# Layer norms turned by VectorE and DMA instead of TensorE, and modulations with the condition as the stationary side

## The chip, the core and the metric

The kernel runs on one core of a Trainium2 chip. A core has five engines with queues of their own: TensorE (matrix products and transposes through its 128x128 array, results into PSUM), VectorE (elementwise work, reductions, 32x32 block transposes), ScalarE (activation functions, copies), GpSimd (called POOL in the profile) and SyncE (SP), which here issues every DMA. Each engine works through its queue in the order of the program, and waits at the head of it for semaphores that others raise. The metric is the device time of one execution in microseconds.

## What is computed

Four blocks of a diffusion transformer follow each other on a batch of 16 samples of 256 tokens with 256 channels, in float32. A condition vector of 256 numbers per sample gives shifts, scales and gates; a context of 77 tokens per sample is attended to. Cut to what matters here:

```python
def ln(x):            # over the 256 channels
    return (x - mean(x)) * rsqrt(var(x) + eps)

# block 0: shift, scale and gate from cond; masked self attention, cross attention, MLP
x = x + g_sa  * (attn(ln(x) * w * (1 + sc) + sh, mask) @ W)
x = x + g_x   * (cross(ln(x) * w * (1 + sc) + sh, ctx) @ W)
x = x + g_mlp * mlp(ln(x) * w * (1 + sc) + sh)
# block 1: x + cross attention of a modulated norm; the context is normed and modulated too
# block 2: self attention (modulated, gated), cross attention (norm alone), MLP (modulated, gated)
# block 3: self attention and cross attention with rotary embedding, MLP; all modulated, no gate
```

with `shift, scale = split(c @ W_mod + b)` and `c` the condition or its silu. Each sample goes through ten norms, so there are 160 in all; nine of the ten kinds have a modulation, and a tenth modulation serves the context of block 1.

## The kernel before

All of x stays in SBUF: `x_sb` holds 16 samples, each as two tiles of 128 tokens by 256 channels, tokens on partitions. The projections need the normed sample with channels on partitions, `xT` (two tiles of 128 channels by 256 tokens).

There are six stages one after the other: attention of block 0 (tiles named a, ac), its MLP (b), the attentions of blocks 1 and 2 (cx, c, cc), the MLP of block 2 (d), the attentions of block 3 (e, ec), and its MLP (f). Within an attention stage some five samples are in work at once. Their number is set by the buffers `kq` (queries and keys, five). An attention consists of a norm, projections (L592, L644, L764), scores for the row maxima (L805, L817), the maxima on VectorE (L831, L835, L839), which are block-transposed, written to DRAM and read back as an extra row of the queries (L851 to L858), scores again for the exponentials (L902, ScalarE L914, L916), the product with the values (L925), a division (L934 to L951) and the output projection with the residual (L972 to L990). An MLP of a sample is a norm, L1015, an activation (L1020) and L972.

The order of the instructions is not written by hand. Every step is entered as a task (`add`, L87) with an engine, a planned duration, the tasks it depends on, and the buffers it takes or uses (`Hold`); `Order.solve` (L104) starts tasks in order of planned time. On TensorE the task with the lowest priority number goes first, on the other engines the one that has been ready longest (with a head start for those that hold a PSUM bank), and a task starts only when its buffers are free by the numbers in `CAPS`. The result is one fixed order per engine. A DMA is a task on SP of 0.45 us (`ISSUE`), with a planned time to landing (`lat`, `mb`).

The norm is `norm_tasks` (L483): VectorE takes mean and variance (L467, L468), GpSimd makes the reciprocal deviation (L473, L474) and the normed sample `xn` (L495), TensorE turns it with four 128x128 transposes into a PSUM bank (L503), and ScalarE writes `xT` from the bank, with the scale and shift of the sample as its per-partition operands (L510, or a plain copy at L507). The modulation is `modulation` (L374): a DMA brings 256x512 weights into half a `kq` buffer (L380), TensorE makes shift and scale for all 16 samples with channels on partitions (L388), eight products in which a 128x128 block of the weights is the stationary side and the condition's 16 columns move, and VectorE adds the bias and the 1 (L393 to L398).

```python
pt = s["pt"] = psum(hm, NC)
for c in range(NC):
    for t in range(NT):
        nc.tensor.transpose(pt[:, c, t * P:(t + 1) * P], s["xn"][:, t, c * P:(c + 1) * P], ident)
```

Of the kernel before, what the change touches and what calls it, by code (L numbers as in the profile page):

```python
# [10 lines left out]
F32 = mybir.dt.float32  # L11
# [202 lines left out]
def pixart_kernel(ctx: ExitStack, tc: tile.TileContext, x, cond_t, ctx_in, mask_c, mask_s, tables, vecs, rows,  # L214
# [6 lines left out]

    CAPS = {"b": 8, "xn": 1, "xT": 2, "kq": 5, "v": 5, "mx": 3, "mr": 2, "ec": 2,
            "ts": 2, "oT": 2, "rope": 2, "qk": 4, "tmp": 2, "gb": 3, "wa": 1, "ctx": 2,
            "cin": 2, "bias": 2, "small": 4, "csmall": 2}

    const = ctx.enter_context(tc.tile_pool(name="const", bufs=1))
    wpool = ctx.enter_context(tc.tile_pool(name="weights", bufs=1))
# [49 lines left out]
    mrs, vs = [], []  # L277
    for j in range(CAPS["mr"]):
        mrs.append(dram.tile([2, 2, 4, 512], F32, name=f"mrow{j}"))

    for j in range(CAPS["v"]):
        vs.append(const.tile([P, NT, H, 32], F32, name=f"vt{j}"))
# [89 lines left out]
    gate_d, gate_t = {}, {}  # L372

    def modulation(name, src, col, shift_at, scale_at, c_t, bias, norm=None, gate=None, deps=(), prio=0, gprio=None):  # L374
        hw, hm, s = Hold("kq"), Hold("b"), {}
        m = mods[name] = const.tile([P, 4, B], F32, name=f"mod_{name}")

        def load():
            s["w"] = kqs[hw.no][:, 0]
            nc.sync.dma_start(s["w"], src[:, :, col:col + 512])  # L380

        def mults():
            ps = psum(hm)
            s["ps"] = ps[:, 0:4 * B].rearrange("p (s b) -> p s b", b=B)
            for i, at in enumerate((shift_at, scale_at)):
                for c in range(NC):
                    for k in range(NC):
                        nc.tensor.matmul(s["ps"][:, 2 * i + c, :], lhsT=s["w"][:, k, at + c * P:at + (c + 1) * P],  # L388
                                         rhs=c_t[:, k, :], start=(k == 0), stop=(k == NC - 1))

        def take():
            v = vec[:, VOFF[bias]:VOFF[bias] + 4].unsqueeze(2).to_broadcast([P, 4, B])
            nc.vector.tensor_tensor(m, s["ps"], v, ALU.add)  # L393
            if norm is None:
                nc.vector.tensor_scalar_add(m[:, 2:4, :], m[:, 2:4, :], 1.0)
            else:
                for c in range(NC):
                    nc.vector.tensor_scalar(m[:, 2 + c, :], m[:, 2 + c, :], 1.0, vcol(norm, c), ALU.add, ALU.mult)  # L398
        t0 = add("SP", ISSUE, load, deps=deps, take=[hw], prio=prio, mb=0.5, lat=2.0)
        t1 = add("PE", 2.0, mults, deps=[t0], take=[hm], use=[hw], prio=prio)  # L400
        mod_t[name] = add("DVE", 0.6, take, deps=[t1], use=[hm], prio=prio)
        if gate is None:
            return
        prio = prio if gprio is None else gprio
        hg = Hold("b")
        g_row, rest = gate
        hr, hw2 = Hold("tmp"), Hold("kq")

        def load2():
            s["wg"] = kqs[hw2.no][:, 0]  # L410
            nc.sync.dma_start(s["wg"][:, :, 0:D], src[:, :, col + 512:col + 768])

        def rowmm():
            pg = s["pg"] = psum(hg)
            nc.tensor.matmul(pg[0:B, 0:D], lhsT=pick(ROW[g_row], B), rhs=row, start=True, stop=False)
            for k in range(NC):
                nc.tensor.matmul(pg[0:B, 0:D], lhsT=c_t[:, k, :], rhs=s["wg"][:, k, 0:D], start=False,
                                 stop=(k == NC - 1))
            if rest is not None:
                bias_row(pg[0:B, D:2 * D], B, *rest)  # L420

        def rowtake():
            d = gate_d[g_row]
            pg, g2 = s["pg"], work.tile([P, NT, D], F32, tag="tmp", bufs=CAPS["tmp"], name=f"g2_{name}")
            nc.vector.tensor_copy(g2[0:B, 0, :], pg[0:B, 0:D])
            if rest is not None:
                nc.vector.tensor_tensor(g2[0:B, 1, :], pg[0:B, D:2 * D], g2[0:B, 0, :], ALU.mult)
            s["g2"] = g2

        def rowout():  # L430
            n = 1 if rest is None else 2
            nc.sync.dma_start(gate_d[g_row], s["g2"][0:B, 0:n, :])
        gate_d[g_row] = dram.tile([B, 1 if rest is None else 2, D], F32, name=f"gate_{g_row}")
        more = () if rest is None or len(rest) == 1 else (rest[3], late_t)
        t2 = add("SP", ISSUE, load2, deps=[*more, *deps], take=[hw2], prio=prio, mb=0.25, lat=2.0)
        t2 = add("PE", 2.2, rowmm, deps=[t2], take=[hg], use=[hw2], prio=prio)
        t3 = add("DVE", 0.8, rowtake, deps=[t2], take=[hr], use=[hg], prio=prio)
        gate_t[g_row] = add("SP", ISSUE, rowout, deps=[t3], use=[hr], prio=prio, mb=0.03, lat=2.0)
# [40 lines left out]
    def join(tasks, prio=0):  # L479
        return add("NO", 0.0, lambda: None, deps=tasks, prio=prio)  # L480

    def norm_tasks(s, b, eps, mod, name, prio, deps=()):

        hs, hn, hm, ht = Hold("small"), Hold("xn"), Hold("b"), Hold("xT")

        def stats():
            s["mv"] = norm_stats(x_sb[:, b], P, NT, name)

        def rstd():
            s["rstd"] = rstd_of(s["mv"], P, NT, eps, name)  # L490

        def scale():
            xn = s["xn"] = work.tile([P, NT, D], F32, tag="xn", bufs=CAPS["xn"], name=f"xn_{name}")
            for t in range(NT):
                nc.gpsimd.tensor_scalar(xn[:, t, :], x_sb[:, b, t, :], s["mv"][:, t, 0:1], s["rstd"][:, t:t + 1],  # L495
                                        ALU.subtract, ALU.mult)

        def turn():
            pt = s["pt"] = psum(hm, NC)
            s["xT"] = work.tile([P, NC, N], F32, tag="xT", name=f"xT_{name}")  # L500
# [4 lines that stand above are left out]
        def take():  # L505
            if mod is None:
                nc.scalar.copy(s["xT"], s["pt"])  # L507
            else:
                for c in range(NC):
                    nc.scalar.activation(s["xT"][:, c, :], s["pt"][:, c, :], AF.Identity,  # L510
                                         scale=mods[mod][:, 2 + c, b:b + 1], bias=mods[mod][:, c, b:b + 1])
        t1 = add("DVE", 1.0, stats, deps=[x_done[b], *deps], take=[hs], prio=prio)
        t2 = add("POOL", 0.95, rstd, deps=[t1], use=[hs], prio=prio)
        t3 = add("POOL", 2.5, scale, deps=[t2], take=[hn], use=[hs], prio=prio)
        t4 = add("PE", 4 * TR, turn, deps=[t3], take=[hm, ht], use=[hn], prio=prio)
        t5 = add("ACT", 0.6 if mod is None else 1.1, take, deps=[t4, mod_t.get(mod)], use=[hm, ht], prio=prio)
        x_done[b] = t3
        return t5, ht

    def early_add(s, b, pre_add, prio):  # L520

# [164 lines left out]
        a = add("PE", NC * nt * TR, turn, deps=deps, take=[hm], use=[h_dst, *hq], prio=prio)  # L686
        return take(lambda: u["p"], a, [hm, h_dst], prio)

    state = {"mr": 0}

    def attention(b, name, n, wv, wkeys, h_w, w_t, eps, mod, half, biases, masked, pre_add, gate, prio, ctxs=None,
                  barrier=None, after=None, norm_deps=()):
# [19 lines left out]
                  joins=[("mx", nm), ("mr", nm)] +  # L712
                        [(i, (nm, g, kc)) for i in ("e", "av") for g in range(NC) for kc in range(nk)])
        admitted.append(x_t)
        xT_t, hx = norm_tasks(s, b, eps, mod, nm, prio, deps=[x_t])

        norms.append(xT_t)
        if self_:
# [631 lines left out]
```

## Time and profile before

| | |
|---|---|
| median of three runs | 2684.58 us (2683.35 to 2687.24) |
| profiled execution, its own time | 2684.49 us |
| its span, first to last instruction | 2682.7 us |
| TensorE busy | 2635.8 us, 98% |
| VectorE, ScalarE, GpSimd busy | 1542.2, 1240.1, 1065.7 us |
| granted TensorE clock, mean | 0.995 |
| norm transposes L503 | 640, 272 or 273 ns each as recorded |
| modulation products L388 | 160 records, 263 ns each in the middle |
| stages: a and ac, b, cx to cc, d, e and ec, f | 642, 239, 761, 232, 576, 233 us |
| DMA, mean | 22 GB/s, 60.25 MB |

In the profile's groups, PE is a matmul and PEld a load of the stationary side; the two overlap, and matmuls overlap each other, so that the duration of one is longer than what it adds to a series. A float32 product is recorded as two matmuls, a transpose as one. "Idle before" is the engine's idle time just before the instructions of a row, with what ended most of it. The chain that ended last is followed back from the last instruction; its shares add up to the span. Buffer numbers are left out of the names.

### The profile page before, as it was taken

How to read it: one execution, taken by the hardware profiler on the slowest of the kernel's cores; microseconds unless marked ns; L12 is line 12 of the kernel's file. 1: busy time of each engine (PE TensorE's matmuls, PEld its weight loads, DVE VectorE, ACT ScalarE, POOL GpSimd, SP SyncE). 2: the span in 40 equal slices, each digit the busy share in tenths (PEclk: the TensorE clock that was granted, in tenths of full speed). 3: DMA queues.
4: the chain of work that ended last, by engine and by line, in shares of the span. 5: the costliest groups of instructions: out<-in, count | busy, mean ns of one | idle time of the engine just before them, and what ended most of it. 6: DMA issues, size and time to landing. Idle time of an engine off the chain costs nothing.

```text
span 2682.7 us, 56475 instructions
## 1 busy us (share of the span) xinstructions
PE 2635.8 (98%) x22144; PEld 1887.2 (70%) x22144; DVE 1542.2 (57%) x4379; ACT 1240.1 (46%) x2495; POOL 1065.7 (40%) x1413
## 2 busy tenths in 40 slices
PE   8999999999999999999999999999999999999999
PEld 5656665766888667666666667888666666667888
DVE  7788886664320566766775664111788876883100
ACT  2444444664332456455555554232455555553332
POOL 4333332545443445133334544433333333562321
PEclk9999999999999999999999999999999999999999
DMA  4000000012110000100000012000000000000000
GB/s 145 14 7 9 10 7 14 16 52 90 31 39 12 25 17 6 35 13 13 20 16 9 5 33 66 16 20 16 11 4 4 4 3 6 5 21 24 20 20 20
DMA packets 53570, 60.25 MB, mean 22 GB/s; under 512 B 19592, under 2 KB 38264, under 8 KB 52536
## 3 DMA queue, kind: packets, MB, share of 16 engines
q1 hardware_dynamic: 53304, 56.65, 7.1%
q8 instruction: 174, 2.85, 0.4%
q14 instruction: 92, 0.75, 0.1%
HBM read 50.44 MB, written 6.19 MB: 21 GB/s over the span
## 4 chain that ended last, share of the span: by engine, by line
PE 92%; DVE 3%; POOL 2%; ACT 1%; issue 1%; DMA 1%; DVEq 0%; ACTq 0%; POOLq 0%; SPq 0%
PE bank L972 20%; PE bank L902 13%; PE bank L1015 12%; PE bank L925 11%; PE bank L805 7%; PE bank L592 7%; PE bank L644 6%; PE bank L764 5%; PE bank L503 3%; PE bank L817 2%; PE bank L684 2%; PE bank L895 2%; PE bank L388 1%; PE bank L579 0%; ACT e_ac L914 0%
## 5 line engine op out<-in xcount | busy, mean ns | idle before, releaser
L902 PE MATMUL bank<-kq 32*128 32x256 f32 (+1 forms) x5120 | 606.2, 396 | 2.9 <-DMA kq<-mrow 2.5
L902 PEld LDWEIGHTS bank<-kq 32*128 32x128 f32 (+1 forms) x5120 | 354.3, 168 | 158.4 <-issue 108.2
L805 PE MATMUL bank<-kq 32*128 32x512 f32 x1536 | 411.1, 638 | 1.9 <-DVE kq L617 1.8
L831 DVE CUSTOM_DVE_ANT_0 junk<-bank,ctxT_masks 128x256 f32<-128x256 f32 x448 | 188.7, 421 | 52.5 <-PE bank L805 21.4
L916 ACT ACTIVATE e_a<-bank 128x512 f32<-128x512 f32 x256 | 137.8, 597 | 175.0 <-PE bank L805 147.1
L916 ACT ACTIVATE e_e<-bank 128x512 f32<-128x512 f32 x256 | 136.1, 599 | 143.9 <-PE bank L805 105.2
L835 DVE TENSOR_REDUCE mx_c<-bank 128x2 f32<-128x512 f32 x256 | 160.2, 681 | 36.8 <-PE bank L805 36.2
L916 ACT ACTIVATE e_c<-bank 128x512 f32<-128x512 f32 x256 | 134.9, 601 | 100.3 <-PE bank L805 74.8
L835 DVE TENSOR_REDUCE mx_e<-bank 128x2 f32<-128x512 f32 x256 | 161.1, 681 | 26.5 <-PE bank L805 25.4
L978 DVE TENSOR_TENSOR x_sb<-x_sb,bank 128x512 f32<-128x512 f32 x80 | 54.8, 685 | 202.3 <-PE bank L972 193.4
L817 PE MATMUL bank<-kq 32*128 32x154 f32 x2048 | 166.9, 309 | 1.3 <-DVE mx_ec L839 0.5
L805 PEld LDWEIGHTS bank<-kq 32*128 32x128 f32 x1536 | 127.4, 184 | 25.2 <-issue 8.1
L817 PEld LDWEIGHTS bank<-kq 32*128 32x128 f32 x2048 | 130.0, 185 | 17.2 <-issue 6.8
L1020 ACT ACTIVATE h_d<-bank,vec 128x256 f32<-128x256 f32 x128 | 53.7, 471 | 156.0 <-PE bank L1015 105.8
L1020 ACT ACTIVATE h_f<-bank,vec 128x256 f32<-128x256 f32 x128 | 53.6, 471 | 153.4 <-PE bank L1015 132.2
L1020 ACT ACTIVATE h_b<-bank,vec 128x256 f32<-128x256 f32 x128 | 53.6, 471 | 146.2 <-PE bank L1015 118.6
L1015 PE MATMUL bank<-xT_b,kq 128*128 128x256 f32 x512 | 113.8, 379 | 0.0
L1015 PE MATMUL bank<-xT_d,kq 128*128 128x256 f32 x512 | 113.6, 380 | 0.0
L1015 PE MATMUL bank<-xT_f,kq 128*128 128x256 f32 x512 | 113.4, 379 | 0.0
L972 PE MATMUL bank<-kq,h_b 128*128 128x256 f32 x512 | 113.2, 379 | 0.0
L972 PE MATMUL bank<-kq,h_d 128*128 128x256 f32 x512 | 113.2, 379 | 0.0
L972 PE MATMUL bank<-kq,h_f 128*128 128x256 f32 x512 | 113.2, 379 | 0.0
(336 smaller groups left out, 5751.4 us busy)
## 6 DMA issues: line engine op xcount, KB each, us to landing
kq<-in_mod_dram SPq DMA_DIRECT2D x10, 512.0 KB
cin<-in_ctx_in_dram SPq DMA_DIRECT2D x36, 128.0 KB
x_sb<-in_x_dram SPq DMA_DIRECT2D x16, 256.0 KB
gb_b<-gate_g0m SPq DMA_DIRECT2D x16, 256.0 KB
gb_c<-gate_g2a SPq DMA_DIRECT2D x16, 256.0 KB
gb_d<-gate_g2m SPq DMA_DIRECT2D x16, 256.0 KB
out_dram<-x_sb SPq DMA_DIRECT2D x16, 256.0 KB
kq<-mrow SPq DMA_DIRECT2D x224, 16.0 KB
```

The source lines that it names most:

```text
L592: nc.tensor.matmul(dst[:, g, :], lhsT=w[:, k, g * P:(g + 1) * P], rhs=xT[:, k, :], start=(k == 0), stop=(k == NC - 1))
L644: nc.tensor.matmul(u["p"][0:r, at:at + D], lhsT=xT()[:, k, t * P:t * P + r], rhs=w()[:, k, :], start=(k == 0), stop=(k == NC - 1))
L805: ls.append(lambda ps=ps, R=R, keys=keys: nc.tensor.matmul(ps.rearrange("p (s k) -> p s k", k=N), lhsT=s["qx"][R, 0, g, t * P:(t + 1) * P] ...
L817: ls.append(lambda ps=ps, R=R, keys=keys, tt=tt: nc.tensor.matmul(ps[:, 2 * tt * n:2 * (tt + 1) * n].rearrange("p (s k) -> p s k", k=n), l ...
L831: nc.vector.tensor_tensor_reduce(junk, u[i][:, i2 * N:(i2 + 1) * N], mb[:, t, :], -1.0, 3.0e38, ALU.add, ALU.min, m[:, i2, g, t:t + 1])
L835: nc.vector.tensor_reduce(m[:, :, g, t], u[i].rearrange("p (s k) -> p s k", k=N), AX.X, ALU.max, negate=True)
L902: (lambda ps=u[i], R=R, q=q: nc.tensor.matmul(ps[0:rows_n, q * N:(q + 1) * N], lhsT=s["kz"][R, q, g, kc * P:kc * P + rows_n], rhs=s["qx"][ ...
L916: nc.scalar.activation(e, u[i][0:rows_n], AF.Exp)
L925: nc.tensor.matmul(u5["p"][32 * r:32 * r + 32, 1 - q, :], lhsT=s["v"][0:rows_n, kc, 8 * g + 2 * r + 1 - q, :], rhs=s["e", g, kc, r][0:rows ...
L972: nc.tensor.matmul(u["p"][:, t, :], lhsT=lhsT(k, t), rhs=w()[:, k, :], start=(k == 0), stop=(k == nk - 1))
L1015: nc.tensor.matmul(u["p"][:, j, :], lhsT=wv["w1"][:, k, f * P:(f + 1) * P], rhs=s["xT"][:, k, :], start=(k == 0), stop=(k == NC - 1))
L1020: nc.scalar.activation(s["h", i][:, j, :], u["p"][:, j, :], func, bias=vcol(b1, 2 * i + j))
```

## The change

The norm keeps its first three steps. Its fourth, the turn on TensorE, stays only where `direct` is true: for the self attention of block 0 and the first two samples (`BY_PE` is 2). Everywhere else four steps take its place. VectorE transposes `xn` in blocks of 32x32 into `y` (one buffer); SP writes `y` to a DRAM tile `yd` (two of them), 128 rows of 2 KB; SP reads it back into `xr` (one buffer) with the blocks in their places, four runs of 512 bytes per partition; and ScalarE writes `xT` from `xr`, in two instructions with or without a modulation. No PSUM bank is held, and `xT` is taken only at the last step.

In the modulation the condition's 16 columns become the stationary side, and the 512 columns of the weights move: two products in place of eight, with the 16 samples on partitions. ScalarE copies the 16x512 result to SBUF (a `tmp` buffer), and four transposes on TensorE bring it into the old layout in a second PSUM bank.

```diff
-        hw, hm, s = Hold("kq"), Hold("b"), {}
+        hw, hr_, hc, hm, s = Hold("kq"), Hold("b"), Hold("tmp"), Hold("b"), {}
...
         def mults():
-            ps = psum(hm)
-            s["ps"] = ps[:, 0:4 * B].rearrange("p (s b) -> p s b", b=B)
+            for k in range(NC):
+                nc.tensor.matmul(psum(hr_)[0:B], lhsT=c_t[:, k, :], rhs=s["w"][:, k, :], start=(k == 0),
+                                 stop=(k == NC - 1))
+
+        def copy():
+            s["r"] = work.tile([P, NT, D], F32, tag="tmp", bufs=CAPS["tmp"], name=f"mr_{name}")
+            nc.scalar.copy(s["r"][0:B].rearrange("b t d -> b (t d)"), psum(hr_)[0:B])
+
+        def turn():
+            s["ps"] = psum(hm)[:, 0:4 * B].rearrange("p (s b) -> p s b", b=B)
+            r = s["r"].rearrange("b t d -> b (t d)")
             for i, at in enumerate((shift_at, scale_at)):
                 for c in range(NC):
-                    for k in range(NC):
-                        nc.tensor.matmul(s["ps"][:, 2 * i + c, :], lhsT=s["w"][:, k, at + c * P:at + (c + 1) * P],
-                                         rhs=c_t[:, k, :], start=(k == 0), stop=(k == NC - 1))
+                    nc.tensor.transpose(s["ps"][:, 2 * i + c, :], r[0:B, at + c * P:at + (c + 1) * P], ident[0:B, 0:B])
...
-        t1 = add("PE", 2.0, mults, deps=[t0], take=[hm], use=[hw], prio=prio)
+        t1 = add("PE", 0.95, mults, deps=[t0], take=[hr_], use=[hw], prio=prio)
+        t1 = add("ACT", 0.6, copy, deps=[t1], take=[hc], use=[hr_], prio=prio)
+        t1 = add("PE", 0.4, turn, deps=[t1], take=[hm], use=[hc], prio=prio)
...
-        t4 = add("PE", 4 * TR, turn, deps=[t3], take=[hm, ht], use=[hn], prio=prio)
-        t5 = add("ACT", 0.6 if mod is None else 1.1, take, deps=[t4, mod_t.get(mod)], use=[hm, ht], prio=prio)
         x_done[b] = t3
-        return t5, ht
+        if direct:
+            t4 = add("PE", 4 * TR, turn, deps=[t3], take=[hm, ht], use=[hn], prio=prio)
+            return add("ACT", 0.6 if mod is None else 1.1, take, deps=[t4, mod_t.get(mod)], use=[hm, ht], prio=prio), ht
+
+        hy, hd = Hold("y"), Hold("yd")
+
+        def turn32():
+            s["y"] = work.tile([P, 4, NT * NC * 32], F32, tag="y", bufs=CAPS["y"], name=f"y_{name}")
+            nc.vector.transpose(s["y"].rearrange("p f (u i) -> p f u i", i=32),
+                                s["xn"].rearrange("p t (c j f) -> p f (t c) j", j=32, f=4))
+
+        def move_out():
+            s["yd"] = yds[state["yd"] % len(yds)]
+            state["yd"] += 1
+            nc.sync.dma_start(s["yd"], s["y"].rearrange("p f n -> p (f n)"))
+
+        def move_in():
+            s["xr"] = work.tile([P, 4, NT, NC, 32], F32, tag="xr", bufs=CAPS["xr"], name=f"xr_{name}")
+            nc.sync.dma_start(s["xr"].rearrange("p a t c i -> p a (t c i)"),
+                              s["yd"].rearrange("(a j) (f n) -> (j f) a n", j=32, f=4))
+
+        def take_in():
+            s["xT"] = work.tile([P, NC, N], F32, tag="xT", bufs=CAPS["xT"], name=f"xT_{name}")
+            for c in range(NC):
+                to = s["xT"][:, c, :].rearrange("p (t a i) -> p t a i", t=NT, a=4)
+                of = s["xr"][:, :, :, c, :].rearrange("p a t i -> p t a i")
+                if mod is None:
+                    nc.scalar.copy(to, of)
+                else:
+                    nc.scalar.activation(to, of, AF.Identity, scale=mods[mod][:, 2 + c, b:b + 1],
+                                         bias=mods[mod][:, c, b:b + 1])
+        hr = Hold("xr")
+        t = add("DVE", 0.7, turn32, deps=[t3], take=[hy], use=[hn], prio=prio)
+        t = add("SP", ISSUE, move_out, deps=[t], take=[hd], use=[hy], prio=prio, lat=2.0)
+        t = add("SP", ISSUE, move_in, deps=[t], take=[hr], use=[hd], prio=prio, lat=2.0)
+        return add("ACT", 1.1, take_in, deps=[t, mod_t.get(mod)], take=[ht], use=[hr], prio=prio), ht
...
-        xT_t, hx = norm_tasks(s, b, eps, mod, nm, prio, deps=[x_t])
+        xT_t, hx = norm_tasks(s, b, eps, mod, nm, prio, deps=[x_t], direct=masked and self_ and b < BY_PE)
```

`CAPS` gains `"y": 1, "yd": 2, "xr": 1`. Because the order is planned from the tasks, the order of every other instruction shifts as well.

## The prediction

> **What bounds the kernel now.** I read the page's first part and its chain, then the chain in order of time, then the row of the line that the change removes, then single moments of the timeline.
>
> ```profile
> PE 2635.8 (98%) x22144; PEld 1887.2 (70%) x22144; DVE 1542.2 (57%) x4379; ACT 1240.1 (46%) x2495; POOL 1065.7 (40%) x1413
> PE 92%; DVE 3%; POOL 2%; ACT 1%; issue 1%; DMA 1%; DVEq 0%; ACTq 0%; POOLq 0%; SPq 0%
> ```
>
> TensorE bounds it: it makes up 92% of the chain that ended last, and in all 40 slices but the first it is busy nine tenths. The removed transposes (L503) hold "PE bank L503 3%" of that chain, 2.5 to 3.5% of 2682.7 us or 67 to 94 us, waits in front of them included; the modulations (L388) hold 1%. What a norm's four transposes cost the array itself is read where nothing else happens, in an MLP stage:
>
> ```profile
> 2643.80 6.91 PE bank L972 x32
> 2650.71 6.91 PE bank L1015 x32
> 2658.05 6.91 PE bank L972 x32
> ```
>
> L1015 ends at 2657.62, and the next sample starts at 2658.05: the four transposes between them take 0.43 us. In the attention stages there is more around them:
>
> ```profile
> its engine sat idle before it (us, times) until:
>   issue: 18.6, 48
>   POOL xn_cx L495: 7.6, 4
>   POOL xn_b L495: 3.6, 4
>   POOL od_c L947: 3.5, 9
> ```
>
> This is L503's own view. "issue" is 0.39 us a time, where the array changes from 32-row tiles to full ones; the others are TensorE standing at the head of its queue until GpSimd has normalised.
>
> [...] L503's row shows 273 as one duration, but the 0.43 us for four show that they overlap, so I count 0.43. [...]
>
> ```profile
> 1161.28 0.32 SPq L540 DMA_DIRECT2D gb_c<-gate_g2a  x1
> 1175.33 0.53 SPq L854 DMA_DIRECT2D mrow<-mt_c  x1
> 1177.32 1.08 SPq L858 DMA_DIRECT2D kq<-mrow  x2
> 1164.34 1.27 POOL L528 TENSOR_TENSOR x_sb<-x_sb,gb_c 128x512 f32<-128x512 f32 x1 [1.77 <-DMA gb_c<-gate_g2a]
> ```
>
> A write to DRAM is followed by its read 1.99 us later; a 256 KB read is in use 3.06 us after its issue.
>
> **The change, part by part**, on the span of 2682.7 us.
>
> 1. Transposes. Ten norms for 16 samples are 160; two (stage a, b below BY_PE = 2) keep the old path. 158 x 0.43 = 68 us leave TensorE's queue. Every stage keeps TensorE above 97% busy, so this is on the path that sets the end: -68.
>
> 2. Waits and mode changes around them. The chain's share says 67 to 94 us, so up to 26 beyond the 68. The order of the changed program has 1391 changes of array mode against 1449; 58 fewer at 0.39 are 23, if none was hidden. Bounds 0 and 26; I take half: -13.
>
> 3. Modulations. Before: eight products in 16 records.
>
> ```profile
> 672.00 1.97 PEld L388 LDWEIGHTS bank<-scondT,kq 128*128 128x128 f32 x16
> 673.89 2.25 PEld L1015 LDWEIGHTS bank<-xT_b,kq 128*128 128x128 f32 x11
> 22.96 0.54 PEld L417 LDWEIGHTS bank<-kq,condT 128*16 128x16 f32 x4 [0.42 <-DMA x_sb<-in_x_dram]
> 23.93 3.32 PEld L644 LDWEIGHTS bank<-w_a,xT_a 128*128 128x128 f32 x16 [0.42 <-ACT xT_a L510]
> ```
>
> From the first weight load to the next line's: 1.89 us each. After: two products of 512 columns. The gate product L417 has the same stationary side and 256 columns: four records in at most 0.97 us (the next load waited for ScalarE as well). Twice the columns: at most 1.94, or 1.73 at the 0.216 of L1015 (6.91/32) per 256. Four small transposes add at most 0.43. So 2.16 to 2.37 against 1.89, times 10: +3 to +5; I take +3. The new ScalarE copy (as L507's 128x512 copy, 0.59) sits between the two TensorE steps; nine modulations are loaded long before use. For the first, the other input is late anyway: GpSimd's norm ends at 12.5 us, the modulation at 11.99 before.
>
> 4. VectorE gains one 128x512 block transpose per norm. L951's 128x256 takes 0.435 from SBUF, L934's 128x512 takes 0.71 from PSUM. The reading here steps by four elements, which no row shows; bounds 0.6 and 1.1, taken 0.71: 158 x 0.71 = 112 us, hidden where VectorE has room. Least room:
>
> ```profile
> 100.00:200.00 100.00, 99.13 (x892) 61.24 (x894) 84.64 (x343) 46.22 (x87) 35.01 (x42) 1.00 0.03 9
> ```
>
> The third number is VectorE: 85% in self-attention of stage a. One norm per 20 us or so adds 0.71, and the stage shortens by some 3%: about 90%. An in-order VectorE that full delays row maxima, whose banks TensorE wants. Bounds 0 and 20 us (all that stages a and ac save); taken +5.
>
> 5. ScalarE reads SBUF in place of PSUM, 2 x 0.567 before. [...] ScalarE is at 46%: 0.
>
> 6. The new chain. VectorE, write, read, ScalarE. A store of 256 KB has its packets done 1.8 us after issue (DMA packets under the out_dram issue), so the write is some 2.0 with the hand-over; the read 3.1 with 512-byte pieces (bounds 2.6 and 4.0); ScalarE 1.15; semaphores and short queueing 0.4. Sum 6.7 us from SP's issue of the write to xT. SP waits for the block transpose, then for the write, and everything behind on SP stands: the write of the row maxima and its read, gate loads, x stores. Each pays only if its own reader is close. SP issues 316 DMAs more, some 0.45 each, on top of some 550 at about 0.5: 420 us of 2600, not full.
>
> Is xT in time? In the changed program's order I sum, for each norm, the TensorE work issued between SP's write and the first matmul on xT, at the before-trace's rates (0.432 for a 256-column product, 0.125 for L902's, 0.137 for L925's, 0.244 for L805's). In the MLP stages it is 16 to 60 us. In the 110 attention norms the middle is 9.5; nine are under 6.7, the smallest 3.8 (c2), 4.2 (c3), 5.2. What is missing below 6.7 sums to 12 us: +12. The same count made for the row maxima of the kernel before, at their 5 us, says 6.7 us; the waits view says
>
> ```profile
> PEld bank L902 <- DMA kq<-mrow: 4.2, 7, 1.3
> PE bank L902 <- DMA kq<-mrow: 2.5, 3, 0.9
> ```
>
> so the count is good to a few us. For the row maxima after, it says 1 us. The waits for xT that exist before (L510's view: matmuls waited 4.0 + 3.0 + 2.9 + 2.3 + 1.4) go where the order no longer has them; I take -10 of these 14.
>
> 7. The PSUM bank that a norm held is freed, and xn (one buffer) is released by VectorE and not by TensorE's queue. POOL waited 137.5 us for L503 in the last MLP; that wait was off the path. 0.
>
> Sum: -68 - 13 + 3 + 5 + 12 - 10 = -71: span 2611.7. The profiled execution's time was 2684.49 with span 2682.7, 1.8 more, and equals the median of the runs (2684.58). Forecast 2613 us.
>
> **Rivals.**
> - A. The waits vanish whole: all 94 us of L503's share go and nothing new comes, 2684.5 - 94 + 3 = 2594, and without the old waits for xT 2584. For: the slack of 9.5 is more than 6.7. Against: nine norms are short.
> - B. VectorE becomes the bound in stages a and e, or the read takes 4 us (sum 7.6): the stalls are 21, not 12, and the VectorE loss 20, not 5. 2613 + 24 = 2637; with a round trip of 8.5 us (37 us of stall) 2653. For: 85% busy before, one in-order queue.
> - C. Slower: the round trip is late everywhere. The same count gives 55 us of stall at 9.0, 88 at 9.7, 105 at 10. The gain before stalls is 83 us (68 + 13 + 10 - 3 - 5), so it decides at 9.6 us, 2.9 more than I have, on every attention norm: SP, held at its head by row-maxima writes or by the block transpose behind VectorE's queue. At 10.5 us the count is 136: 2684.5 - 83 + 136 = 2738. For: the write of one norm and the row maxima alternate in SP's order. Against: the order already leaves 2.45 us for each hop, and TensorE work, not SP, sets the pace.
> - D. It changes nothing: only if transposes were hidden; the MLP chain, where they show as 0.43 gaps, excludes it.
>
> **Chances.** Forecast case (2595 to 2635) 0.62; A (below 2595) 0.12; B (2635 to 2679) 0.18; D (within 0.2%, 2679 to 2690, about what a measurement of this kernel can tell from no change) 0.02; C 0.06. Range for 8 in 10: leaving 0.08 below 2590 and 0.12 above 2655. Faster 0.92.
>
> **What would show it.** MLP periods of 13.82 us (14.25 - 0.43); no L503 rows but eight transposes; modulations of about 2.2 us on TensorE; VectorE's new row near 0.71 us; the read issued about 2 us after the write; TensorE's waits on xT some 12 to 16 us in the attention stages. It is wrong if TensorE's idle time before projections grows past 40 us, if SP's waits move row maxima onto TensorE's path, or if VectorE's maxima show as what ends TensorE's waits in stage a.

## The result and the profile after

The changed kernel takes 2703.7 us (median; 2695.8 to 2706.0) against 2685.8 us of the kernel before on the same chip: a ratio of 1.0062, 95% interval 1.0045 to 1.0079. It is slower by 18 us, where 2613 us was forecast. The profiled execution has a span of 2701.0 us against 2682.7.

The first part of the page and its chain, for the kernel after:

```profile
PE 2619.5 (97%) x21432; PEld 1818.7 (67%) x21432; DVE 1686.9 (62%) x4537; ACT 1256.4 (47%) x2521; POOL 1065.4 (39%) x1413
PE 69%; DVE 5%; DMA 2%; POOL 2%; ACT 1%; issue 1%; SPq 0%; DVEq 0%; ACTq 0%; POOLq 0%
```

TensorE has lost 712 of its 22144 matmul records but only 16 us of busy time; VectorE has gained 145 us. This chain breaks off in stage a: its shares add up to 80%, and the first 530 us are not in it, so that the 69% of TensorE can't be set beside the 92% of before. In the part that it covers, DMA holds 64 us, 58 of them the new writes and reads; the chain of before, over the whole span, held 18 us of DMA.

Several steps came out as forecast. In an MLP stage the chain in order of time shows the period of 2 x 6.91 = 13.82 us, without the 0.43 us gap (start, duration, instructions):

```profile
2590.00 6.91 PE bank L1059 x32
2596.91 6.91 PE bank L1016 x32
2603.82 6.91 PE bank L1059 x32
```

One round trip in stage c, from the timeline (start, duration, engine, line, operation; in brackets the idle time before it and what ended it):

```profile
1243.93 1.11 DVE L535 STREAM_TRANSPOSE y_c<-xn_c 128x512 f32<-128x512 f32 x1 [1.14 <-POOL xn_c L506]
1245.07 0.33 SPq L541 DMA_DIRECT2D yd<-y_c  x1
1247.13 0.37 SPq L545 DMA_DIRECT2D xr_c<-yd  x1
1249.70 1.09 ACT L556 ACTIVATE xT_c<-xr_c,mod_2a 128x256 f32<-128x256 f32 x2 [2.29 <-DMA xr_c<-yd]
1251.16 0.94 PEld L636 LDWEIGHTS bank<-xT_c,w_c 128*128 128x128 f32 x5 [0.45 <-ACT xT_c L556]
```

The read follows the write after 2.06 us, ScalarE follows 2.57 us later, and xT is there at 1250.79, 5.7 us after SP's write, where 6.7 was counted. That is one of the quick ones. Over the 110 attention norms on the new path the middle is 6.6 us, 54 take longer than 6.7, and ten longer than 9.6. A modulation holds TensorE for about 2.2 us, as forecast (the one at 700.48 us: 1.82 for the products, 0.35 for the turns). What was not as forecast is the first line: 1.11 us for a block transpose, not 0.71. It is so in every stage, as L535's own view shows for stage c (durations in ns, shortest, middle and longest):

```profile
L535 DVE STREAM_TRANSPOSE y_c<-xn_c x16: 1079/1108/1116, 1079.8 to 1396.0; 128x512 f32<-128x512 f32 x16
```

TensorE's instructions waited for xT as the views of L510 before and of L556 after list (us, times):

```profile
  PEld bank L592: 4.0, 8
  PEld bank L764: 3.0, 8
  PEld bank L925: 2.9, 8
  PEld bank L644: 2.3, 4
  PE bank L592: 1.4, 1
```

```profile
  PEld bank L636: 19.7, 28
  PE bank L636: 10.0, 6
  PEld bank L808: 3.4, 8
  PEld bank L969: 1.7, 5
  PEld bank L688: 1.3, 4
```

That is 36 us of waits for xT against 13.6 before, where 12 to 16 were expected. For 15.6 of the 26.1 us that loads (PEld) waited, earlier matmuls still ran, so not all of it is lost time.

By stage the span moved like this (boundaries at the first and last MLP product):

| stage | a | b | c | d | e | f |
|---|---|---|---|---|---|---|
| before | 641.9 | 239.2 | 760.5 | 232.2 | 575.8 | 233.1 |
| after | 665.7 | 240.7 | 758.2 | 229.8 | 577.9 | 228.6 |

Stage a alone loses 23.8 us. The others together gain 5.6.

One reading of the trace orders all that follows. I split the span into three: **gaps** (no matmul in execution), **half clock** (half of TensorE's busy time in stretches whose clock record says 0.5: an estimate of what those stretches cost; in the profile after, the matmuls of L636 follow each other there after 427 ns in the middle, and elsewhere after 216), and the **rest**, which is TensorE at work, with the short waits that its overlapping records hide.

| | span | gaps | half clock | rest |
|---|---|---|---|---|
| before | 2682.7 | 46.9 | 12.7 | 2623.2 |
| after | 2701.0 | 81.4 | 29.9 | 2589.7 |
| difference | +18.3 | +34.5 | +17.2 | -33.5 |

These are one profiled execution each, and executions of one kernel differ by some us. So TensorE did get less to do. The saving came back, and more, as gaps and as half clock. Here is one such place, first a line of the timeline of TensorE, then the windows of 3.4 us around it (PE's busy time is the number after the length; the granted clock is the third from the end):

```profile
1316.06 2.61 PE L636 MATMUL bank<-xT_c,w_c 128*128 128x256 f32 x8 [2.05 <-ACT xT_c L556]
```

```profile
1313.90:1317.40 3.50, 1.45 (x10) 1.07 (x7) 2.15 (x5) 2.00 (x5) 0.01 (x1) 1.00 0.25 70
1317.40:1320.80 3.40, 3.40 (x20) 1.83 (x22) 1.05 (x3) 2.06 (x5) 0.48 (x1) 0.50 0.33 82
1320.80:1324.20 3.40, 3.40 (x35) 2.23 (x30) 2.49 (x4) 2.17 (x4) 0.79 (x1) 1.00 0.00 0
```

xT is 2.05 us late; in the next 3.4 us TensorE, busy throughout, gets half its clock (20 matmuls, then 35). By estimate the wait of 2.05 us costs 3.75: its length and half of the 3.4 us.

### The profile page after: what moved, and what is told of

The parts are those of the page before. It is cut to its first block, busy times and chain, and to the rows that moved or that the text cites. A ratio compares the mean times of both kernels' runs of the same rounds, so it can differ in the third digit from the quotient of the medians.

```text
span 2701.0 us, 55663 instructions
## 1 busy us (share of the span) xinstructions
PE 2619.5 (97%) x21432; PEld 1818.7 (67%) x21432; DVE 1686.9 (62%) x4537; ACT 1256.4 (47%) x2521; POOL 1065.4 (39%) x1413
## 4 chain that ended last, share of the span: by engine, by line
PE 69%; DVE 5%; DMA 2%; POOL 2%; ACT 1%; issue 1%; SPq 0%; DVEq 0%; ACTq 0%; POOLq 0%
PE bank L1016 18%; PE bank L1059 12%; PE bank L946 9%; PE bank L969 8%; PE bank L636 6%; PE bank L849 5%; PE bank L808 3%; PE bank L688 3%; PE bank L861 2%; PE bank L728 1%; DMA xr_c<-yd 1%; DVE mx_e L879 1%; DMA yd<-y_c 1%; PE bank L386 0%; DMA yd<-y_b 0%
## 5 line engine op out<-in xcount | busy, mean ns | idle before, releaser
L946 PE MATMUL bank<-kq 32*128 32x256 f32 (+1 forms) x5120 | 613.1, 399 | 2.9 <-DMA kq<-mrow 0.6
L879 DVE TENSOR_REDUCE mx_c<-bank 128x2 f32<-128x512 f32 x256 | 159.7, 679 | 16.1 <-PE bank L849 15.1
L1059 PEld LDWEIGHTS bank<-xT_d,kq 128*128 128x128 f32 x512 | 97.0, 190 | 14.6 <-issue 1.6
```

The costliest lines, as they stand in the source:

```text
L879: nc.vector.tensor_reduce(m[:, :, g, t], u[i].rearrange("p (s k) -> p s k", k=N), AX.X, ALU.max, negate=True)
L946: (lambda ps=u[i], R=R, q=q: nc.tensor.matmul(ps[0:rows_n, q * N:(q + 1) * N], lhsT=s["kz"][R, q, g, kc * P:kc * P + rows_n], rhs=s["qx"][ ...
L1059: nc.tensor.matmul(u["p"][:, j, :], lhsT=wv["w1"][:, k, f * P:(f + 1) * P], rhs=s["xT"][:, k, :], start=(k == 0), stop=(k == NC - 1))
```

## The experiments

My theories after the result: 1, VectorE's longer block transpose delays row maxima and so the banks that TensorE wants; 2, the round trip makes xT late; 3, in the attention stages the transposes had not been what sets the pace; 4, added later, the planner's order is better or worse by accident; 5, added last, gaps cost clock.

### The transposes and the new path, in a fixed order

In these four the planner's input is unchanged, so every engine keeps its order and the instructions named are missing. Two of them also give `xn` three buffers in place of one: the first, in which ScalarE reads `xn` itself, and the one with the moves alone, in which SP writes `xn` itself; what those buffers alone are worth was not tested.

The kernel before without the transposes:

```diff
+            if name not in ("a0", "a1"):
+                s["pt"] = s["xn"]
+                return
             pt = s["pt"] = psum(hm, NC)
```

> The kernel before in its own order on every engine, with the 158 norms' transposes on TensorE left out; ScalarE takes the normalised tile itself in place of the turned one (so the values of everything behind are not the reference's), still after GpSimd has made it. It prices what the removed transposes are worth to the kernel before when nothing takes their place. Forecast's own theory (they lie on the path everywhere): 81 us less, about 2604 us. Theory 3 (only in the MLP stages TensorE sets the pace; in the attention stages the pace is set by the loop through VectorE and ScalarE that empties the banks): 48 x 0.43 = 21 us less, about 2664 us.

Measured: 2643.9 us, ratio 0.9848 (0.9832 to 0.9863): 41 us, half of the 81 of the forecast's steps 1 and 2 and twice what theory 3 said. The split (always of the profiled execution) says by stage where it paid:

| | transposes, at 0.43 us a norm | rest | gaps | half clock | span |
|---|---|---|---|---|---|
| MLP stages b, d, f (48 norms) | 20.6 | -19.2 | +0.1 | 0 | -19.1 |
| attention stages a, c, e (110 norms) | 47.3 | -41.8 | +11.3 | +11.8 | -18.7 |

In the MLP stages nearly the whole price is gained. In the attention stages most of the work does go, but more than half of that comes back, as gaps and as half clock, and some 6 us were hidden in TensorE's records from the start. How that can be hidden is seen where self-attention samples follow each other: six samples of self-attention in stage e, between the ends of the same two projections, look like this:

```profile
2030.80:2163.60 132.80, 132.69 (x1229) 87.43 (x1232) 106.33 (x222) 68.53 (x132) 44.50 (x60) 1.00 0.02 4
```

```profile
2006.20:2138.60 132.40, 132.02 (x1204) 85.53 (x1208) 106.36 (x222) 68.86 (x132) 44.42 (x60) 1.00 0.02 4
```

(windows of the kernel before, then of this one.) 24 transposes are gone and the stretch is 0.4 us shorter, not 2.6; and TensorE is "busy" for 99.9% of it with them and 99.7% without. The timelines of the same place in both:

```profile
2049.10 0.69 PE L503 MATMUL bank<-ident,xn_e 128*128 128x128 f32 x4
2049.16 0.76 POOL L947 TENSOR_TENSOR od_e<-ts_e,rec_e 128x128 f32<-128x128 f32 x2
2049.96 0.45 DVE L951 STREAM_TRANSPOSE oT_e<-od_e 128x256 f32<-128x256 f32 x1
2050.89 1.59 PEld L972 LDWEIGHTS bank<-w_e,oT_e 128*128 128x128 f32 x8 [0.43 <-issue]
```

```profile
2024.53 0.76 POOL L950 TENSOR_TENSOR od_e<-ts_e,rec_e 128x128 f32<-128x128 f32 x2
2025.32 0.45 DVE L954 STREAM_TRANSPOSE oT_e<-od_e 128x256 f32<-128x256 f32 x1
2026.25 1.59 PEld L975 LDWEIGHTS bank<-w_e,oT_e 128*128 128x128 f32 x8 [0.74 <-ACT xT_e L513]
```

The projection L972 (L975) starts 1.73 and 1.72 us after GpSimd's product with the reciprocals has started. That chain, GpSimd, VectorE, projection, keeps its own pace at this place, and the transposes had stood in its shadow. "POOL od_c L947" in L503's own view, which the prediction read as GpSimd's norm, is this product in stage c. Theory 3 holds here, not everywhere.

The changed kernel's order without the new path, as below; then with the block transposes put back alone, and with the moves put back alone, which then carry `xn`. In the first two, xT waits for nothing, not even for the norm:

```diff
         def turn32():
+            return
         def move_out():
-            nc.sync.dma_start(s["yd"], ...)
         def move_in():
-            nc.sync.dma_start(s["xr"]..., s["yd"]...)
+            s["xr"] = still...
```

> The changed kernel in its own order on every engine, with the block transposes on VectorE and both moves left out; ScalarE's copy into xT reads a tile that never changes (so the values are not the reference's), and xT waits for neither the norm nor the moves. It shows what the changed order would take if the new path cost nothing. Forecast's theory, and theories 1 and 2, which put the loss on VectorE's block transpose or on the round trip: about 2600 us (2585 to 2620). Theory 3 (the transposes were not what set the pace of the attention stages): 2655 to 2680 us.

> As the run before this one, with the block transposes put back on VectorE, where they cost their 1.10 us each and release the normalised tile, but without the moves and with xT waiting for none of it (values not the reference's). Theory 1 (VectorE's 174 us delay row maxima in its one queue and so the banks that TensorE wants): most of the loss is back, 2680 us or more. Theory 2 (the round trip through DRAM makes xT late): within 15 us of the run without them. Theory 3: some 20 to 30 us above the run without them.

> The changed kernel in its own order with the block transposes on VectorE left out and both moves kept: SP writes the normalised tile to DRAM and reads it back, and xT waits for that (the 32x32 blocks are not turned, so the values are not the reference's). Theory 1: near the run without both parts, within 15 us. Theory 2: close to the changed kernel, 2685 us or more. If both matter, the two single parts add up to what the changed kernel has more than the run without both.

| | time | ratio to before (95%) |
|---|---|---|
| neither | 2666.3 | 0.9932 (0.9910 to 0.9954) |
| block transposes | 2674.3 | 0.9961 (0.9946 to 0.9976) |
| moves | 2683.2 | 0.9995 (0.9986 to 1.0004) |
| both: the changed kernel | 2703.7 | 1.0062 (1.0045 to 1.0079) |

With a path that costs nothing the changed order is still 22 us slower than the order of before without transposes. That was in no theory. The block transposes cost 8, the moves 17, and together they cost 37, 12 more than their sum. The four times of "neither" run from 2660 to 2675 us, so the 22 and the 8 are good to some 6 us; the 12 are 10 when they are taken from the ratios, and with all four intervals good to some 9. It would fit that only with both does the block transpose delay the write, which is not shown. Neither theory 1 nor theory 2 alone gives the 37 us; theory 2 alone gives about half.

### The parts, and the planner's numbers

The old norms with the new modulations; the new norms with the old modulations; the new norms in the MLP stages only (with the old modulations); and the changed kernel with measured durations in its planner:

```diff
-        t = add("DVE", 0.7, turn32, ...
-        t = add("SP", ISSUE, move_out, ..., lat=2.0)
-        t = add("SP", ISSUE, move_in, ..., lat=2.0)
+        t = add("DVE", 1.1, turn32, ...
+        t = add("SP", ISSUE, move_out, ..., lat=1.5)
+        t = add("SP", ISSUE, move_in, ..., lat=2.4)
```

> The kernel before with the modulations changed and every norm turned by TensorE as before. Forecast: +3 us, 2688 us. If new tasks push the planner's order about, which the run without both parts suggests (22 us longer than the kernel before without its transposes, in the changed order), up to +20 us.

> The changed kernel with the old modulations (16 small products each) and the new norms. If the norms carry the loss: 2695 to 2710 us, as the changed kernel. If the new modulations carry the 22 us that the changed order loses: 2675 to 2685 us.

> The kernel before with the new path in the 48 norms of the MLP stages alone; the attention stages' norms are turned by TensorE, the modulations are the old ones. The runs so far give the MLP stages as the only place where a period falls by the transposes' whole 0.43 us (13.82 against 14.25), with 16 to 60 us of other work to cover the round trip: 19 us less, about 2666 us. If the planner's order of the attention stages is upset by it as well: 2675 us or more.

> The changed kernel with the planner told what the trace shows: 1.1 us for the block transpose in place of 0.7, and latencies that make the write 2.05 us and the read 2.85 us from issue to use. If the loss comes from an order written for a too cheap block transpose and too cheap a read: 2670 to 2685 us. If the loss is in the work itself, or the order moves by as much for any change of its inputs: within 10 us of the changed kernel, 2695 to 2715 us.

| | time | ratio (95%) | gaps | half clock | rest |
|---|---|---|---|---|---|
| modulations only | 2694.3 | 1.0034 (1.0021 to 1.0047) | 47.4 | 12.3 | 2636.6 |
| norms only | 2667.2 | 0.9935 (0.9920 to 0.9950) | 68.4 | 16.1 | 2578.4 |
| norms of the MLP stages only | 2680.9 | 0.9987 (0.9978 to 0.9996) | 54.0 | 32.5 | 2601.8 |
| changed kernel, planner's numbers | 2670.4 | 0.9944 (0.9927 to 0.9960) | 56.8 | 19.4 | 2591.8 |

The new norms alone make the kernel faster by 18 us; with the modulations, worth 9 us by themselves, they make it 18 us slower. And the whole change, with three numbers of its planner altered, is 15 us faster than before. The MLP run shows the split at work: its rest falls by 21.4 us, close to 48 x 0.43 = 20.6, and half clock takes 19.8 back, in the attention stages, where only the order has changed. Its profiled execution took 2690.1 us, though, 9 above the median, at the lowest clock of its twelve (0.987; the others 0.990 to 0.993), so that in most executions half clock takes less.

So does the order swing for any change of the planner's inputs? One number altered in the kernel before (0.125 for 0.109 us for a transpose), one in the kernel after (1.2 for 0.95 us for the wide products), and the measured numbers with the norms alone:

```diff
-    TR = 0.109
+    TR = 0.125
```

> The kernel before with one number of the planner changed, 0.125 us in place of 0.109 for a transpose on TensorE: the same instructions in another order. Theory 4 (the planner's greedy order swings by tens of microseconds for any change of its inputs, so the changed kernel's loss in stage a is an accident of its order): at least 8 us away from 2685, to either side. If the order is robust and the loss belongs to the change: 2680 to 2690 us.

> The changed kernel with one number of the planner changed, 1.2 us in place of 0.95 for the modulations' two products (the trace has 2 x 0.591): the same instructions in another order. Theory 4: at least 10 us off the changed kernel, most likely faster, 2665 to 2695 us. If the new modulations themselves cost the 36 us that lie between the changed kernel and the one with the new norms alone: 2698 to 2710 us.

> The new norms with the old modulations, and the planner told the measured 1.1 us for the block transpose and the measured latencies of write and read. If right numbers make the better order: 2650 to 2662 us. Theory 4: anywhere within 15 us of the 2667 us of the same work with the first numbers, and as likely above it as below.

Measured: 2697.5 us (1.0045, 1.0031 to 1.0060), 2681.3 us (0.9984, 0.9973 to 0.9996) and 2659.9 us (0.9911, 0.9894 to 0.9928). The same instructions in another order move the kernel before by +14 us and the changed one by -22. So the order alone moves the time, as theory 4 says. That it does so by accident is not shown. The number changed in the kernel before went away from what its trace shows (0.43 / 4 = 0.108 us), and the time rose; the numbers altered in the changed kernel, here and in the table above, and in the one with the new norms alone went towards the measured ones, and the time fell each time (by 22, 33 and 7 us). That a planner orders better when its numbers are right fits these four as well. No run moved a number of the changed kernel the wrong way. For the kernel before, the split says what has changed (its span is 2699.5): gaps 41.8, half clock 33.6, rest 2624.1. The work is the same, the gaps are 5 us less, and half clock costs 21 us more. The last of the three is the fastest kernel of this study: all of the norms' change, none of the modulations'. Its 7 us over the norms with the first numbers are less than the swing.

### Is it the modulations' work or the order?

The changed order with the old products (sixteen as recorded), and the order of the norms alone with the new ones. The first diff, in its main lines; the second puts the new products, with the copy and the turns behind them, in the place of the old ones:

```diff
 # the changed kernel: wide products -> sixteen small ones; the turns back fall away
-                nc.tensor.matmul(psum(hr_)[0:B], lhsT=c_t[:, k, :], rhs=s["w"][:, k, :], ...)
+                        nc.tensor.matmul(ps[:, 2 * i + c, :], lhsT=s["w"][...], rhs=c_t[:, k, :], ...)
```

> The changed kernel in its own order on every engine, with the sixteen small products of the old modulation put where the two wide ones stand; ScalarE's copy stays and the four turns back fall away, so all results are computed. If the 36 us between the changed kernel and the one with the new norms alone are the order's: 2698 to 2710 us, as the changed kernel. If they are the work of the new modulations: 2670 to 2685 us.

> The order of the kernel with the new norms alone, with the new modulations (two wide products, ScalarE's copy, four turns back) put where the sixteen small products stood, so that the whole change is there; TensorE stands still while ScalarE copies, 10 times some 1.0 us. If the 36 us are the order's: 2667 + 10 x (1.0 + 0.3) = 2680 us at most. If they are the work of the new modulations: 2700 us or more.

Measured: 2701.9 us (1.0075, 1.0059 to 1.0092) and 2672.6 us (0.9958, 0.9945 to 0.9971). The new products in place of the old ones move the time by +2 us in the one order and +5 in the other; exchanging the order moves it by 31 to 35. The runs compared here come from different chips; by the ratios, each to the kernel before on its own chip, it is -4 and +6 against 28 to 38. The work costs nothing clear of noise in the first order and some 5 us in the second; the order is what counts. Where the orders differ is seen in stage a. Windows over it: the kernel after, its order with the old products, the other order with the new ones:

```profile
0.00:665.70 665.70, 634.96 (x5938) 380.01 (x5938) 509.56 (x1737) 315.80 (x579) 261.56 (x358) 0.98 0.18 57
```

```profile
0.00:665.00 665.00, 634.70 (x5962) 386.00 (x5962) 509.54 (x1737) 315.20 (x579) 261.00 (x358) 0.98 0.19 57
```

```profile
0.00:630.70 630.70, 609.50 (x5939) 371.62 (x5939) 507.00 (x1738) 315.54 (x579) 260.64 (x357) 1.00 0.20 60
```

First and last do the same work (VectorE 509.56 and 507.00 us, ScalarE 315.80 and 315.54), 35.0 us apart. The split gives gaps 30.7 against 21.2, half clock 8.7 against none, rest 626.3 against 609.5. Counting the time that passes up to each matmul's end, the 35 us are spread: 8.6 on the products with the values, 7.3 on those of the key mask, 6.9 on the scores for the row maxima, less than 4 on each other kind. It is many small waits and no single one; which of the planner's choices makes them is not settled.

### Two smaller questions

The block transposes without moves, reading 32 columns side by side:

```diff
-        s["xn"].rearrange("p t (c j f) -> p f (t c) j", j=32, f=4))
+        s["xn"].rearrange("p t (c f j) -> p f (t c) j", j=32, f=4))
```

> The changed order with the block transposes on VectorE and without the moves (values not the reference's), as an earlier run, but each block transpose reads its 32 columns side by side and not four elements apart. If the step in the reading is what makes it 1.10 us and not 0.71: 0.70 to 0.86 us each. If a transpose of 128x512 within SBUF costs that anyhow: 1.05 us or more.

```profile
L538 DVE STREAM_TRANSPOSE y_c<-xn_c x16: 668/711/715, 1065.0 to 1369.1; 128x512 f32<-128x512 f32 x16
```

0.71 us against 1.10: the reading in steps of four elements costs the 0.39 us. It took 2667.7 us, 7 below the 2674.3 with the stepped reading; a single time without an interval, it settles nothing on the whole.

The fastest kernel with stage a's, and with all, self-attention norms back on TensorE:

```diff
-                          direct=masked and self_ and b < BY_PE)
+                          direct=masked and self_)       # the second: direct=self_
```

> The kernel with the new norms, the old modulations and the planner's numbers as measured (2660 us), with the 16 self-attention norms of stage a turned by TensorE as before, where VectorE has least room. If VectorE's block transposes cost time there: stage a shorter than its 638.5 us by up to 10 us. If not, or if the order's swing is larger than that: within 10 us to either side.

> As the run before this one, with all 48 self-attention norms (stages a, c, e) turned by TensorE and the new path in the cross-attention and MLP norms. The first run says that taking the transposes out gains nothing while self-attention samples follow one another; then the time is that of the kernel with all norms on the new path or better, 2645 to 2662 us. If they do count there: 48 x 0.43 = 21 us slower, 2675 us or more.

Measured: 2669.0 us (0.9949, 0.9934 to 0.9964; stage a 640.7 us against 638.5) and 2672.7 us (0.9960, 0.9947 to 0.9973). Neither is better than 2659.9, but 9 and 13 us lie within the order's swing: where the new path should be used is left open.

### Do gaps cost clock?

Gaps put into stage d of the kernel before, in sixteen short pieces and in five long ones of about the same sum:

```diff
+                if name == "d" and i == 2 and b >= 0:       # long: b % 3 == 2
+                    for z in range(1):                      # long: range(5)
+                        nc.vector.tensor_tensor(s["xT"], s["xT"], s["xT"], ALU.max)
```

> The kernel before, in its own order, with a short gap of TensorE put into each of the 16 MLP samples of stage d: between a sample's second and third product group VectorE replaces xT by the larger of xT and xT, which is xT, and TensorE waits for it, about 0.95 us, in all 15 us. Theory 5 (besides their own length, gaps cost half of TensorE's clock for the next 3.4 us, but only where TensorE stood for more than about half of a 3.4 us window of the clock's): the clock in stage d stays whole, 2685 + 15 = 2700 us. If every gap halves the clock: 2700 + 16 x 1.7 = 2727 us.

> The same with the same sum of gaps in fewer pieces: five of the 16 samples of stage d get five such operations in a row, a gap of about 3.35 us each, in all 17 us. Theory 5: each gap brings one or two windows of 3.4 us at half clock with it, 5 x 1.7 to 5 x 3.4 us more, so 2685 + 17 + 8 to 17 = 2710 to 2719 us, and the clock's record shows them right behind the gaps. If gaps cost only their own length: 2702 us, and no half-clock window in stage d.

Measured: 2705.1 us (1.0067, 1.0050 to 1.0084) and 2714.4 us (1.0108, 1.0093 to 1.0123). The waits of TensorE in stage d, short and long:

```profile
PE bank L1018 <- DVE xT_d L1014: 14.4, 16, 1.4
```

```profile
PE bank L1018 <- DVE xT_d L1014: 18.8, 5, 3.8
```

Stage d is 250.9 us and 264.1 us long, 18.7 and 31.9 more than the 232.2 us without gaps. The short gaps, 14.4 us in all, brought no half clock in that stage; the other 4.3 us are in the rest. Each of the five long ones did, for 3.4 or 6.8 us, 27.3 us in all, which cost 12.0; 18.8 + 12.0 is nearly all of the 31.9. Two of the five, in the windows of the run with long gaps:

```profile
1676.70:1683.50 6.80, 5.75 (x14) 4.59 (x15) 1.30 (x3) 0.84 (x2) 0.00 (x0) 0.50 0.00 0
1683.50:1727.90 44.40, 41.91 (x208) 36.78 (x206) 7.46 (x20) 11.97 (x28) 17.66 (x18) 1.00 0.06 18
1727.90:1734.70 6.80, 5.54 (x13) 4.46 (x14) 1.51 (x3) 0.84 (x2) 0.00 (x0) 0.50 0.01 2
```

Theory 5 holds as far as this goes: the short gaps cost no clock and the long ones do. Where between 0.9 and 3.8 us it begins these two runs don't say; the count at the end does.

## Why the prediction was wrong

The sum of the forecast beside what the runs in a fixed order showed, in us:

| step | forecast | measured |
|---|---|---|
| 1, 2: transposes, and waits around them | -81 | -41 |
| 3: modulations; the order itself | +3 | +22 |
| 4: VectorE | +5 | +8 |
| 6: round trip, less the old waits for xT | +2 | +17 |
| 4 and 6 together, beyond their sum | 0 | +12 |
| sum | -71 | +18 |

The measured column follows one way from the kernel before to the changed one, so it adds up by construction; its parts are good to some 6 us each, and the 12 to some 9.

**Steps 1 and 2 failed, in one sentence**: "Every stage keeps TensorE above 97% busy, so this is on the path that sets the end". The price of 0.43 us was right: 61 us of work went for 158 norms, where 68 was counted, and the MLP period is 13.82 us. But the engine, busy as it is, was done sooner by the whole of that work only in the MLP stages. In the attention stages 47 us of transposes were worth 18.7: TensorE then waited for other engines, 11.3 us more in gaps and 11.8 in half clock. Some 6 us had been hidden in TensorE's records, which overlap (four transposes of 273 ns each take 0.43 us): in the stretch of self-attention looked at they cover 99.9% of the time with the transposes and 99.7% without, and the chain through GpSimd and VectorE set the pace. The 13 us of step 2 were counted as waits that go; none of that gain is seen. Rival D was dismissed because the MLP chain shows the gap, which is where all of the saving counts.

**Step 3**: +3 us agrees with the work as far as it can be told (-4 to +6 us when the order is kept). What no step held is that the new tasks make the planner write another order: some 22 us at once, with moves of 7 to 33 us for changed numbers. The count of slack that I made in the new order asked only whether xT is in time; it didn't ask whether the order was as good as the old one in all else. In a kernel whose order is planned, that is a term of the sum.

**Step 4** was mis-sized at the row: 1.10 us and not 0.71, inside its bounds of 0.6 and 1.1, 174 us of VectorE and not 112. The loss of 8 us by itself lies near the 5 taken, which is luck: the row was half as long again as counted, and the 8 are no better known than to 6 us. Rival B had this mechanism, but set its 24 us against a gain that was not there.

**Step 6** had the durations right (2.06 us to the read; 6.6 us in the middle of the 110, where 6.7 was counted) and the waits too small: 36 us in place of 12 to 16, and long ones cost clock besides (the one of 2.05 us shown above, 3.75 by the estimate). The 0.4 us for semaphores and short queueing within the 6.7 was an estimate of mine, read from no row. The count took one figure for all norms, but half of them took longer than it. Rival C had the right sign and this mechanism, but not its size and not its place: ten of the 110 took longer than the 9.6 us from which it was to decide, and while those ten were on their way TensorE stood for 0.2 us in all. Six of them, of 29 to 39 us, had been issued in an MLP stage, long before they were needed.

**Clock.** No step priced a wait at more than its length. In the profiled executions half clock costs 17 us more than before, about as much as the kernel has lost.

**Step 5** and **step 7** stand: ScalarE's copies with a modulation took 0.60 us from SBUF (592 to 599 ns in the middle, by tile, at L556) against 0.57 from PSUM (564 to 578 at L510), though they also read in another pattern; and no loss was found there.

## What to carry to other kernels

A busy share near 100% does not say that time falls with the work: leave the work out in a fixed order and see what comes back, as gaps and as half clock. Where an order is planned, compare a change within one order and over several, as here the order alone was worth more than the change; and give the planner measured numbers, which went with the faster kernels here, though the cause is not shown. And price a wait of TensorE by the clock as well: in the MLP stage sixteen gaps of 0.9 us cost 18.7 us, five of 3.8 us cost 31.9.

## What was not expected of the hardware

- In both profiles the half-clock stretches start on one grid of 3.4133 us: in the profile after, starts as far apart as 378.8, 1317.4 and 2460.9 us all leave 3.3 when divided by it, as do all twelve; in the profile before, all six leave 1.3. Over the 20 profiles, of the grid's windows at full clock in which TensorE stood for 1.8 us or more, 55 of 56 were followed by half clock; with 1.0 to 1.8 us, 49 of 133; with less than 1.0 us, 54 of 15063. In the profiles before and after alone it is 9 of 9, 5 of 14 and 4 of 1513, counted from the first clock record on (at 18.3 and 16.9 us). So in these runs about half a window of standing still was enough: the gap of 2.05 us, which fell within the window from 1314.0 to 1317.4 us, was followed by half clock, and cost 3.75 by the estimate above.
- Standing still is not the whole of it: the 54 are a third of the half-clock stretches counted. In six profiles with the old modulations one of them follows a window that holds a modulation's products, in which TensorE never stood. In the kernel before (a line of the timeline, then the windows; the first has 46 matmuls at full clock, the next 23 at half):

```profile
943.99 1.96 PE L388 MATMUL bank<-scondT,kq 128*128 128x16 f32 x16
```

```profile
943.40:946.80 3.40, 3.40 (x46) 2.41 (x36) 1.71 (x6) 2.17 (x6) 2.54 (x4) 1.00 0.03 5
946.80:950.20 3.40, 3.40 (x23) 2.04 (x20) 2.24 (x9) 1.20 (x3) 1.69 (x4) 0.50 0.11 28
```

What brings half clock here is not shown.
- VectorE's block transposes of 128x512 within SBUF took 0.71 us reading side by side (694 to 711 ns in the middle, by tile), and 1.10 us reading every fourth element (1100 to 1108 in the changed kernel).
